# Four small re-orderings in a four-layer gated cross-attention kernel: a copy moved in ScalarE's queue, two PSUM tiles taken from another pool, the last additions reordered with one on GpSimd, and one split moved behind a transpose

## The chip, the cores and the metric

The kernel runs on one core of one Trainium2 chip, in one launch. The metric is device microseconds (us) from the start of the execution to its end; of three timed executions the median counts. The core has a matmul engine (TensorE, PE in the profile; its weight loads are listed apart as PEld), VectorE (DVE), ScalarE (ACT), GpSimd (POOL), and SyncE (SP), which here only issues DMAs. Every engine works through its own list of instructions in order, and waits at an instruction until the semaphores that it names have been counted up by others.

## The reference

Two batches of 256 tokens with 256 features (512 tokens in all, four tiles of 128) pass through four layers, each of them a gated cross-attention to a context of 512 rows per batch and then a gated feed-forward:

```python
x = x + tanh(g_xattn[l]) * xattn_l(layernorm(x), ctx)
x = x + tanh(g_ffn[l])   * ffn_l(layernorm(x))
```

Layer 0 has 16-head attention without projections and a feed-forward with ternary weights; layer 1 has 16 heads of width 128 with query, key, value and output projections, and a dense gated feed-forward; layer 2 has linear attention and a mixture of 8 experts of which each token uses one; layer 3 has one-head attention with a mask, and a mixture of 8 experts of which each token uses two (160 slots per expert), beside a shared feed-forward that all tokens use. Everything is float32.

## The kernel before

The 512 tokens live in one SBUF tile `x` of 128 partitions by four tiles by 256 features. The whole kernel is one straight program. Its engines' orders are set partly by the text (the helpers `inline`, with the lists `line`, `pool_line` and `pe_line`, keep DVE's, POOL's and PE's instructions of a stretch in the order in which the text writes them), partly by a scheduler that fills in the rest, and in places by `behind(i, j, reason)`, which tells the scheduler to place instruction `i` after instruction `j` on the same engine, without a semaphore. Tiles come from pools; a pool gives out a buffer again once its last readers are done, so a new tile makes its first writer wait for them. The PSUM pools that matter here are `ps_acc` (2 buffers, tag `acc`), `ps_mm` (4 buffers, tag `mm`, taken by `mm()`) and `ps_tr` (2 buffers, tag `tr`).

Four places are touched.

**Context parts (lines 602 to 623).** For layer 1 the turned context `ctxT` is split into a rounded part `ctx_top` and the scaled rest `ctx_rest`, so that products of full precision can be built from faster matmuls. The generator `context_parts` does this in four pieces (two batches by two feature halves), one at a time, between other work. A piece is: DVE cuts the low bits off (`cut`), ACT copies the result to `ctx_top` (line 614), DVE takes the difference (line 618), ACT scales it into `ctx_rest[:, 0]` (line 619), and one step later DVE forms `ctx_rest[:, 1]` from it (line 621). The fourth piece falls into the change from layer 0 to layer 1, where PE turns the four normalized token tiles (line 255), ACT copies each to `xT` (line 792, `turned_x`), PE computes two heads' first keys (`whole_keys`, `keys_step`, with ACT's copies in lines 776 and 796), and then the first two query products, which read the whole of `xT`. The list `copied` holds the copy of the last turned tile; only `top` is put behind it.

**Layer 2's experts (lines 1586 to 1676).** Tokens are gathered into slots of 32 rows, four of which make a `quad`; there are six quads. The loop over `q` runs `l2_up(q)`, then for the quad before `l2_mask(q - 1)` and `l2_down(q - 1)`, then `l2_turn(q)`, then `homeward`, which sends finished quads' rows back to the tokens with matmuls into `y`. `l2_down` ends by splitting its result in two halves: DVE cuts `top2` (line 1621), ACT copies it (line 1623), DVE subtracts (line 1624). `l2_turn` has PE turn `h` into a `tr` tile and `evict` copy it to `hT` on DVE and ACT by turns (lines 203 to 206); for quad 5 it is ACT's turn.

**Layer 3's experts (lines 1930 to 2016).** Ten quads of 128 slots in five pairs. `l3_up`, `l3_turn` and `l3_down` follow each other; `l3_down(q)` accumulates in a tile `acc` of `ps_acc`, `evict` copies it to SBUF (DVE and ACT by turns), and GpSimd scatters the rows to a table `yg` in DRAM with an indirect DMA (line 1847). The last pair, quads 8 and 9, is followed on PE by `shared_down(0)` to `shared_down(3)`, the shared feed-forward's output for the four token tiles, also in `acc`.

**The end (lines 2016 to 2042).** Once all ten scatters have landed, four DMAs (two from SP's queue, two from ACT's) read the table back, for each token its two rows: `rows[n]`. DVE adds, for each token tile `n`, the shared part (`add_to_x(n, accs[n], gf(3))`) and, in `final(n)`, the two rows (k = 0 and 1) with their weights `kept`; tile 3's rows go through PE instead, with `spread`. `store(n)` issues the output's DMA from SP. After the last instruction each engine reads the flag `bad`, branches past a fallback that is not taken here, and meets the others at a barrier.

Of the kernel before, what the change touches and what calls it, by code (L numbers as in the profile page):

```python
# [17 lines left out]
F32 = mybir.dt.float32  # L18
# [3 lines left out]
AF = mybir.ActivationFunctionType  # L22
# [3 lines left out]
P = 128  # L26
NT = 4
D = 256
# [11 lines left out]
EPS = 2.0 ** -12  # L40
# [10 lines left out]
def flamingo(ctx: ExitStack, tc: tile.TileContext, a: dict, out: bass.AP):  # L51
    nc = tc.nc

    def pool(name, bufs, space=None):
        kw = {} if space is None else {"space": space}
        return ctx.enter_context(tc.tile_pool(name=name, bufs=bufs, **kw))
# [4 lines left out]
    q1 = pool("q1", 4)  # L61
    small = pool("small", 6)
    ps_acc = pool("ps_acc", 2, bass.MemoryType.PSUM)


    x = const.tile([P, NT, D], F32, name="x")
# [37 lines left out]
    def pair(i, name, dtype=F32):  # L104
        return slab.tile([P, 2, WCOLS], dtype, tag=f"p{i}", name=name)
# [84 lines left out]
    def gf(layer):  # L190
        return tg[:, 4 + layer : 5 + layer]


    def behind(i, j, reason):

        tc.add_manual_dep(i.ins, j.ins.name, mybir.DependencyInfo(
            mybir.DependencyClass.NoSync, mybir.DependencyReason.DATA), reason=reason)
# [24 lines left out]
    def inline(i, line=line):  # L222
        if line:
            if line[-1] is not None:
                behind(i, line[-1], "in the order of the text")
            line[:] = [i]
        return i

    def norm_stats(n):

        st = small.tile([P, 6], F32, tag="st", name="st", bufs=4)
        mv = small.tile([P, 2], F32, tag="mv", name="mv", bufs=4)
        rstd = small.tile([P, 1], F32, tag="rstd", name="rstd", bufs=4)
        inline(nc.vector.bn_stats(st, x[:, n, :]))
        inline(nc.vector.bn_aggr(mv, st))  # L235
        inline(nc.gpsimd.tensor_tensor(rstd, mv[:, 1:2], eps_ln, ALU.add), pool_line)  # L236
        inline(nc.gpsimd.tensor_tensor(rstd, rstd, less_half, ALU.pow), pool_line)
        return mv[:, 0:1], rstd
# [40 lines left out]
    def mm(shape=None):  # L279
        return ps_mm.tile(shape or [P, 512], F32, tag="mm", name="mm")  # L280
# [5 lines left out]
    def add_to_x(n, acc, scalar, cols=slice(0, D)):  # L286
        return inline(nc.vector.scalar_tensor_tensor(x[:, n, cols], acc, scalar, x[:, n, cols], ALU.mult, ALU.add))  # L287
# [230 lines left out]
    mixed, acc, es, stats = {}, {}, {}, {}  # L518
    for s in range(18):
        n = s // 4  # L520
# [21 lines left out]
        if s % 4 == 2 and s < 16:  # L542
# [4 lines left out]
            if n == 0:  # L547
                rest = [norm_stats(m) for m in (2, 3)]
# [45 lines left out]
    def cut(dst, src):  # L594

        return nc.vector.tensor_scalar(dst.bitcast(I32), src.bitcast(I32), -4096, None, ALU.bitwise_and)

    ctx_top = nat.tile([P, B, 2, M], F32R, tag="nat", name="ctx_top")
    ctx_rest = pair(3, "ctx_rest", F32R).rearrange("p i (b k m) -> p i b k m", b=B, k=2)
# [4 lines left out]
    def context_parts():  # L604

        w = pair(5, "ctx_w").rearrange("p i (b k m) -> p i b k m", b=B, k=2)
        for b in range(B):
            for k in range(2):
                last = yield
                src = ctxT[:, b, k, :]  # L610
                t, l = (w[:, i, b, k, :] for i in range(2))
                i = cut(t, src)
                behind(i, last, "in turn, where there is room")
                top = nc.scalar.copy(ctx_top[:, b, k, :], t)
                for c in copied:
                    behind(top, c, "not among the turned tiles")
                copied.clear()
                nc.vector.tensor_sub(l, src, t)
                nc.scalar.mul(ctx_rest[:, 0, b, k, :], l, 1.0 / EPS)
                last = yield  # L620
                i = nc.vector.tensor_sub(ctx_rest[:, 1, b, k, :], t, ctx_rest[:, 0, b, k, :].bitcast(F32))
                behind(i, last, "in turn, where there is room")
        yield
# [317 lines left out]
    for h in range(16):  # L941
# [9 lines left out]
        for b in range(B):  # L951
# [12 lines left out]
            if h and h % 2 == 0:  # L964
                if b == 0:
                    sums1 = l1_sums([totals.pop((h - 2 + i, c)) for i in range(2) for c in range(B)])
                else:
                    scale = l1_turned(sums1)
# [23 lines left out]
            if hl and g < 3:  # L992
                n = 2 * (hl - 1) + b
# [9 lines left out]
    scale = l1_turned(sums1, 3)  # L1003
# [4 lines left out]
    t = totals.pop((15, 1))  # L1008
# [15 lines left out]
    scale = l1_scales(sums, 2)  # L1024
# [282 lines left out]
    t = negatives(early)  # L1307
# [63 lines left out]
    def rtile(shape=(P, NT, E), dtype=F32):  # L1371
        return small.tile(list(shape), dtype, tag=f"r{len(shape)}", name="route", bufs=12)
# [47 lines left out]
    turned = [logits2(n) for n in range(2)]  # L1420
# [37 lines left out]
    turned = []  # L1458
# [42 lines left out]
    t, u = rtile(), place  # L1501
# [45 lines left out]
    t = rtile()  # L1547
# [52 lines left out]
    def l2_turn(q, h):  # L1600
        n = 4 if q < 5 else 2
        hT = q2.tile([P, n, P], F32, tag="q2", name="hT2")
        tr = ps_tr.tile([P, n, P], F32, tag="tr", name="tr")
        for c in range(n):
            inline(nc.tensor.transpose(tr[:, c, :], h[:, c * P : (c + 1) * P], ident), pe_line)
        evict(hT, tr)
        return hT

    def l2_down(q, hT):
        acc = ps_tr.tile([P, D], F32, tag="tr", name="acc2")  # L1610
        n = 4 if q < 5 else 2
        for c in range(n):
            for j in range(4):
                at = c if q < 5 else j % 2 * n + c
                inline(nc.tensor.matmul(acc[j * BLK : (j + 1) * BLK, :], lhsT=hT[:, c, j * BLK : (j + 1) * BLK],  # L1615
                                        rhs=dn2[home(q, j)][:, at * D : (at + 1) * D], start=(c == 0), stop=(c == n - 1)), pe_line)
        if q < 3:
            reload_dn2(q)

        top = q1.tile([P, D], F32, tag="q1", name="top2")  # L1620
        nc.vector.tensor_scalar(top.bitcast(I32), acc.bitcast(I32), -4096, None, ALU.bitwise_and)
        o = kept_back[q][:, 1, :].rearrange("p (i d) -> p i d", i=2) if q < 4 else q2.tile([P, 2, D], F32R, tag="q2", name="o2")
        nc.scalar.copy(o[:, 0, :], top)
        nc.vector.tensor_sub(o[:, 1, :], acc, top)
        return o
# [24 lines left out]
    hTs, os, backs = {}, {}, {}  # L1650
# [9 lines left out]
    for q in range(QUADS + 1):  # L1660
        if q < QUADS:
            h = l2_up(q)
        if q == 0:
            second_rows()
        if 1 <= q <= QUADS:
            backs[q - 1] = l2_mask(q - 1)
            os[q - 1] = l2_down(q - 1, hTs.pop(q - 1))

        if q == 5:
            dn3 = [load(half, f"l3_dn{k}") for k, half in enumerate(halves_of(5, "dn3"))]  # L1670
            sh = [load(half, f"l3_sh{k}") for k, half in enumerate(halves_of(0, "sh3"))]
            gu3 = [load(half, f"l3_gu{k}") for k, half in enumerate(halves_of(3, "gu3") + halves_of(4, "gu3"))]
        if q < QUADS:
            hTs[q] = l2_turn(q, h)
        if 2 <= q < QUADS:
            homeward([(q - 2, 0)])
        if q == 5:
            homeward([(0, 1), (1, 1)])
        if q == QUADS:
            homeward([(4, 0), (2, 1), (3, 1), (4, 1)])  # L1680
            load_table(AF.Exp, silus[0], "the table of exponentials")
# [114 lines left out]
    es, t = l3_exps(0, ps3[0])  # L1796
# [107 lines left out]
    kept = const.tile([P, 2, NT], F32, name="kept")  # L1904
# [8 lines left out]
    def shared_down(n, more=[]):  # L1913
        acc = ps_acc.tile([P, D], F32, tag="acc", name="acc")
        chain(acc, [(hS[c // 2][:, c % 2, n * P : (n + 1) * P], shd[:, c, :]) for c in range(6)] + more)
        return acc
# [5 lines left out]
    for g in range(5):  # L1922
        t = q4.tile([P, 2, D + 1], F32, tag="q4", name="xg_sb")
# [33 lines left out]
        return hT  # L1957

    def l3_down(q, hT):
        acc = ps_acc.tile([P, D], F32, tag="acc", name="acc")  # L1960
        for c in range(2):
            for j in range(4):
                e = (4 * q + j) * BLK // CAP
                dw = dn3[e // 4].rearrange("p (e c d) -> p e c d", e=4, d=D)[:, e % 4, c, :]
                inline(nc.tensor.matmul(acc[j * BLK : (j + 1) * BLK, :], lhsT=hT[:, c, j * BLK : (j + 1) * BLK], rhs=dw,
                                        start=(c == 0), stop=(c == 1)), pe_line)
        o = q2.tile([P, D], F32, tag="q2", name="o3")
        evict(o, acc)
        scatter(yg, slots[q // 2][:, q % 2, D : D + 1].bitcast(I32), o, 2 * T - 1, returned)
# [26 lines left out]
    hs, hTs = {}, {}  # L1996
# [20 lines left out]
    accs = [shared_down(n) for n in range(2)]  # L2017
    rows = []
# [4 lines left out]
        rows.append(o)  # L2023

    def final(n):
        for k in range(2):
            add_to_x(n, rows[n][:, k, :], kept[:, k, n : n + 1])

    def store(n):
# [2 lines left out]
    for n in range(2):  # L2032
        add_to_x(n, accs[n], gf(3))
    accs = [shared_down(2), shared_down(3, [(spread[:, k, :], rows[3][:, k, :]) for k in range(2)])]
    final(0)
    store(0)
    add_to_x(2, accs[0], gf(3))
    for n in (1, 2):
        final(n)
        store(n)  # L2040
# [659 lines left out]
```

## Time and profile before

| | |
|---|---|
| timed runs, median (lowest to highest) | 546.95 us (546.9 to 547.33) |
| profiled execution, its own time | 548.4 us |
| its span from the first to the last instruction | 546.7 us |
| mean clock granted to TensorE | 0.997 |
| PE busy | 535.6 us, 98% |
| DVE, ACT, POOL busy | 61%, 43%, 23% |

The profile has a page (busy times, the span in slices, the chain of work that ended last, the costliest groups of instructions) and answers on parts of the trace. In a row of the timeline the columns are start and duration in us, engine, line, operation, the tile written and the tiles read, shapes, and how many instructions of the same kind the row merges; in brackets is the engine's idle time before it, and what ended that. The end of a matmul is modelled. The names `l_`, `w`, `acc` and the like are the program's tiles without their numbers, so that `acc2`, for one, is shown as `acc`.

### The profile page before, as it was taken

The page shows a single profiled execution, that of the slowest core. Times are in us where ns is not written, and L with a number is a line of the kernel's source. Part 1 is how long each engine was busy: PE and PEld are TensorE (multiplying, and loading weights), DVE is VectorE, ACT ScalarE, POOL GpSimd, SP SyncE. Part 2 cuts the span into 40 slices and gives each one's busy share as a digit, 9 for nine tenths or more (in the row PEclk, how much of TensorE's full clock was granted, in tenths as well). Part 3 has the DMA queues.
Part 4 walks back from the last instruction along what each step waited for, and adds up shares of the span by engine and source line. Part 5 has one row for each costly group of instructions (what it writes and reads, how often), then busy time and mean ns, then how long its engine had stood idle before and what let it go on. Part 6 is the DMA issues. An engine that isn't in the chain of part 4 may idle for free.

```text
span 546.7 us, 8723 instructions
## 1 busy us (share of the span) xinstructions
PE 535.6 (98%) x3304; PEld 394.6 (72%) x3304; DVE 333.3 (61%) x778; ACT 237.4 (43%) x487; POOL 124.1 (23%) x228
## 2 busy tenths in 40 slices
PE   8999999999999999999999999999999999999995
PEld 6554774878888888887888888687776447884464
DVE  5999797745556454754547567765477526562323
ACT  7886465644354434444344533551333212421320
POOL 5676104111021110311012223212022002252150
PEclk9999999999999999999999999999999999999998
DMA  8920130000004000040000404699040899413013
GB/s 265 424 67 0 25 129 1 1 1 0 1 0 151 4 2 1 1 153 1 0 1 1 155 0 155 230 316 375 22 153 1 309 398 291 174 48 121 19 50 127
DMA packets 15528, 57.06 MB, mean 104 GB/s; under 512 B 2653, under 2 KB 5924, under 8 KB 12102
## 3 DMA queue, kind: packets, MB, share of 16 engines
q1 hardware_dynamic: 13718, 51.61, 26.0%
q0 software_dynamic: 1472, 4.28, 2.3%
q8 instruction: 28, 0.46, 0.4%
q10 hardware_dynamic: 288, 0.52, 0.3%
q14 instruction: 22, 0.18, 0.1%
HBM read 51.60 MB, written 5.25 MB: 104 GB/s over the span
## 4 chain that ended last, share of the span: by engine, by line
PE 85%; DVE 5%; DMA 3%; issue 2%; POOL 2%; ACT 1%; SPq 1%; POOLq 0%; DVEq 0%
PE mm L284 26%; PE acc L284 18%; PE mm L643 9%; PE mm L645 4%; PE mm L1589 4%; PE q L643 2%; PE s L464 2%; PE mm L1943 2%; PE acc L1615 2%; DMA w<-in_l_gate 2%; PE gu L643 2%; PE acc L476 1%; PE outT L720 1%; PE q L645 1%; PE mm L1413 1%
## 5 line engine op out<-in xcount | busy, mean ns | idle before, releaser
L284 PE MATMUL mm<-qT,kT 128*128 128x256 f32 x256 | 60.7, 381 | 0.0
L284 PE MATMUL acc<-e,v 128*128 128x256 f32 x256 | 60.6, 379 | 0.0
L284 PEld LDWEIGHTS mm<-qT,kT 128*128 128x128 f32 x256 | 48.1, 190 | 9.3 <-ACT oT L835 1.6
L284 PEld LDWEIGHTS acc<-e,v 128*128 128x128 f32 x256 | 48.3, 189 | 8.2 <-issue 0.4
L631 POOL TENSOR_TENSOR h_parts<-w,h_top 128x256 fp32r<-128x256 f32 x28 | 20.8, 744 | 139.9 <-PE acc L284 73.6
L824 ACT ACTIVATE e<-mm 128x512 f32<-128x512 f32 x64 | 38.1, 598 | 22.3 <-PE mm L284 22.1
L827 DVE TENSOR_TENSOR t<-e,e 128x512 f32<-128x512 f32 x32 | 22.1, 690 | 24.4 <-ACT e L824 24.2
L468 ACT ACTIVATE e<-s 128x512 f32<-128x512 f32 x64 | 32.9, 605 | 6.0 <-PE s L464 5.8
L236 POOL TENSOR_TENSOR rstd<-mv,eps_ln 128x1 f32<-128x1 f32 x31 | 6.8, 219 | 109.4 <-DVE mv L235 109.3
L648 ACT ACTIVATE v<-mm 128x512 f32<-128x512 f32 x24 | 14.3, 597 | 31.1 <-PE mm L645 31.1
L643 PE MATMUL mm<-ctx_top,h_parts 128*128 128x512 f32 x56 | 27.3, 488 | 0.0
L284 PE MATMUL acc<-w,oT 128*128 128x256 f32 x112 | 26.8, 381 | 0.1
L835 ACT COPY oT<-acc 128x256 f32<-128x256 f32 x32 | 11.9, 372 | 34.2 <-PE acc L284 34.2
L649 DVE SCALAR_TENSOR_TENSOR v<-mm,v 128x512 f32<-128x512 f32 x24 | 16.6, 692 | 16.6 <-ACT v L648 16.6
L648 ACT ACTIVATE kT<-mm 128x512 f32<-128x512 f32 x28 | 16.7, 598 | 20.5 <-PE mm L645 20.5
L287 DVE SCALAR_TENSOR_TENSOR x<-acc,gsum,x 128x256 f32<-128x256 f32 x56 | 23.6, 476 | 2.8 <-PE acc L284 2.2
L649 DVE SCALAR_TENSOR_TENSOR kT<-mm,kT 128x512 f32<-128x512 f32 x28 | 19.3, 688 | 6.7 <-ACT kT L648 6.7
L284 PEld LDWEIGHTS acc<-w,oT 128*128 128x128 f32 x112 | 20.1, 190 | 3.5 <-ACT oT L835 0.5
L643 PE MATMUL mm<-v_parts,ctx_top 128*128 128x512 f32 x48 | 22.2, 462 | 0.0
L464 PE MATMUL s<-w_q,ctx_nat 32*128 32x256 f32 x256 | 21.6, 401 | 0.5 <-ACT e L468 0.2
L643 PE MATMUL mm<-ctx_rest,h_parts 128*128 128x512 f32 x56 | 22.0, 393 | 0.0
L649 DVE SCALAR_TENSOR_TENSOR qT<-q,qT 128x512 f32<-128x512 f32 x14 | 9.7, 691 | 18.4 <-ACT qT L648 18.4
(438 smaller groups left out, 1180.6 us busy)
## 6 DMA issues: line engine op xcount, KB each, us to landing
gu<-in_l_gu_all SPq DMA_DIRECT2D x14, 1024.0 KB, 7.3
w<-in_l_all SPq DMA_DIRECT2D x4, 2048.0 KB, 8.4
dn<-in_l_dn_all SPq DMA_DIRECT2D x4, 1024.0 KB, 6.3
dn<-in_l_dn_all SPq DMA_DIRECT2D x6, 512.0 KB, 8.6
gu<-in_l_gu SPq DMA_DIRECT2D x4, 704.0 KB, 17.5
ctxT<-in_ctxT SPq DMA_DIRECT2D x4, 512.0 KB, 11.6
ctx_nat<-in_ctx SPq DMA_DIRECT2D x3, 512.0 KB, 7.9
dn<-in_l_dn SPq DMA_DIRECT2D x2, 704.0 KB
```

The costliest lines, as they stand in the source:

```text
L284: inline(nc.tensor.matmul(dst, lhsT=lhsT, rhs=rhs, start=(i == 0), stop=(i == len(pairs) - 1)), pe_line)
L287: return inline(nc.vector.scalar_tensor_tensor(x[:, n, cols], acc, scalar, x[:, n, cols], ALU.mult, ALU.add))
L464: in_turn(nc.tensor.matmul(ps[j][:, k, :], lhsT=ctx_nat[rows, b, hf, c * P : (c + 1) * P], rhs=qm[rows, n, i, :], start=True, stop=True))
L468: exps.append(nc.scalar.activation(es[j], ps[j], AF.Exp))
L631: nc.gpsimd.tensor_sub(dst[1], src, t)
L643: inline(nc.tensor.matmul(same, lhsT=left(i, k), rhs=right(i, k), start=(k == 0 and i == 0), stop=(k == 1 and i == 1)), pe_line)
L645: inline(nc.tensor.matmul(cross, lhsT=left(2, k), rhs=right(2, k), start=(k == 0), stop=(k == 1)), pe_line)
L648: nc.scalar.mul(dst, cross, -EPS * scale)
L649: return inline(nc.vector.scalar_tensor_tensor(dst, same, (1.0 + EPS) * scale, dst, ALU.mult, ALU.add))
L824: nc.scalar.activation(e, s, AF.Exp)
L827: nc.vector.tensor_add(t, es[0], es[1])
L1589: inline(nc.tensor.matmul(ps[j * BLK : (j + 1) * BLK, :], lhsT=xsT[k][:, block * BLK : (block + 1) * BLK], rhs=gu2[home(q, j)][:, at : at ...
```

## The change

1. In `context_parts` the difference and the scaling into `ctx_rest[:, 0]` are written ahead of the loop over `copied`, and the scaling too is put `behind` the copies of turned tiles. In the built program ACT's order changes for the fourth piece alone: the scaling moves from between the second and third `xT` copies to behind the fourth copy and the `ctx_top` copy, past three copies. DVE's order is the same.
2. `l3_down` takes its tile from `mm()` for quads 8 and 9, and from `ps_acc` for the others, as before. PE's order is the same; the waits of the first matmuls of quad 8, quad 9, `shared_down(0)` and `shared_down(1)` change with the buffers.
3. At the end, `add_to_x(2, ...)` (the shared part of tile 2) is written ahead of `final(0)`; `final` takes k = 1 before k = 0; and for tile 2, k = 1, ACT scales the row into a new tile `row2` and GpSimd adds that to `x`. DVE has one instruction fewer, ACT and POOL one more each.
4. `l2_down` now returns its PSUM tile, and the split in halves is a function of its own, `l2_halves`. For all quads it follows at once, but for quad 4 it follows `l2_turn(5)`. On ACT, the copy of the turned tile of quad 5 now stands before the copy of quad 4's half; DVE's order is the same.

```diff
@@ context_parts
                 top = nc.scalar.copy(ctx_top[:, b, k, :], t)
+                nc.vector.tensor_sub(l, src, t)
+                rest = nc.scalar.mul(ctx_rest[:, 0, b, k, :], l, 1.0 / EPS)
                 for c in copied:
                     behind(top, c, "not among the turned tiles")
+                    behind(rest, c, "not among the turned tiles")
                 copied.clear()
-                nc.vector.tensor_sub(l, src, t)
-                nc.scalar.mul(ctx_rest[:, 0, b, k, :], l, 1.0 / EPS)
@@ l2_down
         if q < 3:
             reload_dn2(q)
 
+        return acc
+
+    def l2_halves(q, acc):
         top = q1.tile([P, D], F32, tag="q1", name="top2")
...
@@ the loop over quads
-            os[q - 1] = l2_down(q - 1, hTs.pop(q - 1))
+            acc = l2_down(q - 1, hTs.pop(q - 1))
+            if q != 5:
+                os[q - 1] = l2_halves(q - 1, acc)
...
         if q < QUADS:
             hTs[q] = l2_turn(q, h)
+        if q == 5:
+            os[q - 1] = l2_halves(q - 1, acc)
@@ l3_down
-        acc = ps_acc.tile([P, D], F32, tag="acc", name="acc")
+        acc = ps_acc.tile([P, D], F32, tag="acc", name="acc") if q < 8 else mm([P, D])
@@ final
-        for k in range(2):
+        for k in (1, 0):
+            if (n, k) == (2, 1):
+                t = q1.tile([P, D], F32, tag="q1", name="row2")
+                nc.scalar.activation(t, rows[n][:, k, :], AF.Copy, scale=kept[:, k, n : n + 1])
+                nc.gpsimd.tensor_add(x[:, n, :], x[:, n, :], t)
+                continue
             add_to_x(n, rows[n][:, k, :], kept[:, k, n : n + 1])
@@ the last additions
     accs = [shared_down(2), shared_down(3, [(spread[:, k, :], rows[3][:, k, :]) for k in range(2)])]
+    add_to_x(2, accs[0], gf(3))
     final(0)
     store(0)
-    add_to_x(2, accs[0], gf(3))
     for n in (1, 2):
```

## The prediction

> **What bounds the kernel.** I read the page first (busy times, then the chain that ended last), then the timeline around each of the four edits.
>
> ```profile
> span 546.7 us, 8723 instructions
> PE 535.6 (98%) x3304; PEld 394.6 (72%) x3304; DVE 333.3 (61%) x778; ACT 237.4 (43%) x487; POOL 124.1 (23%) x228
> ...
> PE 85%; DVE 5%; DMA 3%; issue 2%; POOL 2%; ACT 1%; SPq 1%; POOLq 0%; DVEq 0%
> ```
>
> PE is busy for 535.6 of 546.7 us, and the chain is PE's for 85%. So a gap closed in PE's row ahead of the last stage moves everything behind it, as long as nothing with a time of its own stands there. In the busy times by stage, PE has 229.92 of the 230 us from 100 to 330 us, and 41.83 of the 42 from 420 to 462. From 519.6 us on the chain leaves PE: scatters on POOL, their landing, the rows' DMAs, DVE's additions, the stores. There PE's gaps are worth nothing by themselves.
>
> The timeline of the first place:
>
> ```profile
> 89.35 0.37 ACT L792 COPY xT<-tr 128x256 f32<-128x256 f32 x1 [0.44 <-PE tr L255]
> 90.01 0.75 PE L255 MATMUL tr<-ident,xn 128*128 128x128 f32 x4
> 90.59 1.88 PE L284 MATMUL mm<-ctxT,w 128*128 128x512 f32 x4
> 91.30 0.63 ACT L619 ACTIVATE ctx_rest<-ctx_w 128x512 fp32r<-128x512 f32 x1 [1.58 <-DVE ctx_w L618]
> 91.83 0.57 ACT L796 COPY kT<-mm 128x512 f32<-128x512 f32 x1
> 92.30 0.65 ACT L792 COPY xT<-tr 128x256 f32<-128x256 f32 x2
> 93.00 1.12 PE L284 MATMUL q<-xT,w 128*128 128x512 f32 x2 [0.53 <-ACT xT L792]
> ```
>
> ACT stands idle for 1.58 us at the scaling of the fourth piece, which waits for DVE, while the third and fourth tiles, turned by 90.76, stay uncopied behind it, and PE at last waits for the copies.
>
> The second place, quad 4 and quad 5 of layer 2:
>
> ```profile
> 454.99 0.96 PE L1643 MATMUL y<-back 128*128 128x256 f32 x6
> 455.39 0.41 ACT L1623 CAST o<-top 128x256 fp32r<-128x256 f32 x1 [1.15 <-DVE top L1621]
> 455.71 0.36 ACT L206 COPY hT<-tr 128x256 f32<-128x256 f32 x1
> 456.12 1.07 PE L1615 MATMUL acc<-dn,hT 128*32 128x256 f32 x16 [0.17 <-ACT hT L206]
> ```
>
> ACT copies the half first, though the tile that PE waits for was turned earlier (454.80 + 0.44 = 455.24 in the same timeline).
>
> The end:
>
> ```profile
> 526.53 0.42 DVE L204 COPY o<-acc 128x256 f32<-128x256 f32 x1 [1.51 <-PE acc L1965]
> 527.00 1.93 PE L1965 MATMUL acc<-dn,hT 88*32 88x256 f32 x32 [0.36 <-DVE o L204]
> 528.50 0.97 POOL L1847 DMA_INDIRECT yg<-o,xg_sb  x1 [0.30 <-issue]
> 529.77 0.97 POOL L1847 DMA_INDIRECT yg<-o,xg_sb  x1 [0.30 <-issue]
> 530.72 0.37 ACT L206 COPY o<-acc 128x256 f32<-128x256 f32 x1 [3.63 <-remote]
> 531.36 0.97 POOL L1847 DMA_INDIRECT yg<-o,xg_sb  x1 [0.62 <-issue]
> 538.07 1.01 DVE L287 SCALAR_TENSOR_TENSOR x<-o3g,kept,x 128x256 f32<-128x256 f32 x2 [3.09 <-DMA o3g<-yg]
> 539.39 1.91 DVE L287 SCALAR_TENSOR_TENSOR x<-o3g,kept,x 128x256 f32<-128x256 f32 x4
> 541.22 0.48 DVE L287 SCALAR_TENSOR_TENSOR x<-acc,tg,x 128x256 f32<-128x256 f32 x1
> ```
>
> Scatters follow each other by 1.27 us (528.50, 529.77); only the last comes later, 1.59 us behind. Quad 9's eviction on ACT started at 530.72 though its matmuls end at 528.93 by the trace. I have no cause for these 1.8 us; other evictions start some 0.1 us after their matmuls.
>
> **Part 1, the scaling.** No work goes away; a 0.63 us scaling passes three copies on ACT. Before: four key matmuls from 90.59, pitch (1.88 - 0.59) / 3 = 0.43, so the first query matmul was due at 92.31; it came at 93.00, and its pair took 1.12 instead of 0.59 + 0.43 = 1.02. That is 0.69 + 0.10 = 0.79 us. After: ACT is free from 89.72; the `kT` copy waits for keys that end at 90.17, then two `xT` copies at the 0.28 between them: about 91.4, ahead of 92.31. So PE has no gap: **-0.79**. Bounds: the gap in the row alone, 0.53, and 0.79; I take 0.79, the distance of starts. What is late next: the scaling ends at about 92.45 instead of 91.93, and DVE's L621 waits for it. L621 already took 1.69 us there (0.684 in its median row), since POOL's subtraction ran from 91.83 for 1.27; it really could work only from 93.1 on, so 0.5 us later costs nothing. Behind it, DVE's first sum that PE needs (L827) starts at 100.42 after 1.23 us of idleness, which covers the 0.79. Nothing else with its own time stands in the way: the loads of that stretch were issued by 65.99 us and landed by 74.18.
>
> **Part 4, the halves.** The order on ACT is turned: the `hT` copy can start at 455.30 and ends at 455.66, and six `y` matmuls (last start 455.67, pitch 0.12) let PE go on at 455.79 instead of 456.12: **-0.33**. Bounds 0.17 (the gap in the row) and 0.33. The half of quad 4 is copied 0.3 us later, at about 456.03, and read by PE at 457.12 - 0.33 = 456.79: covered. DVE's order is unchanged. SP's loads of layer 3 follow PE here and landed by 471.75, far ahead of their use.
>
> **Part 2, the last experts.** Quad 8's matmuls no longer wait for quad 6's eviction (0.36 idle, 527.00 instead of about 526.46), `shared_down(0)` no longer for quad 8's; PE is 0.5 to 0.8 us earlier there, off the chain. On the chain, quad 8's scatter is bound by POOL's pitch from quad 6's (527.23), which does not move. Only the last scatter gains: 529.77 + 1.27 = 531.04 instead of 531.36, **-0.32**, if quad 9's eviction ends by 530.8; due at 528.46, it could again be 1.8 late (530.3 + 0.37) and still make it. Bounds: -0.32, and +0.6 if it is held until after the next scatter has been made (531.3 + 0.37 + 0.27 for POOL's start is 531.96).
>
> **Part 3, the last additions.** One 0.40 us step (the shared part of tile 2, at 539.00) moves ahead of the rows' landing, where DVE idles 3.09 us: covered. Another, 0.49 us, leaves DVE, and becomes ACT 0.4 (L1623's 0.41, a 128x256 cast) and POOL 0.73, the nearest row for an addition of this shape, L566:
>
> ```profile
> L566 POOL TENSOR_TENSOR all_r<-all_r,r x4: 727/730/1382, 27.9 to 55.5; 128x256 f32<-128x256 f32 x4
> ```
>
> Tile 2's row is the second DMA on SP's queue, issued at 534.69 and landing 3.7 to 4.5 us on, some 538.8; ACT ends at 539.25, POOL can start at about 539.4 to 539.5 (0.1 to 0.27 for a start behind a semaphore). DVE then runs tile 0 at 538.07 and 538.59, tile 1 at 539.00 and 539.50 to 539.99, all with two SBUF inputs. The maximum of the row above, 1382, lies beside such a DVE instruction, and L621 stretched to 1.69 beside POOL; so the two take turns. Either POOL goes second: 539.99 to 540.72, tile 2's last row at 540.79, tile 3's part at 541.19 (before: 541.22). Or first: tile 3's part at 540.99. **-0.1** between them. Bounds -0.55 (no turns taken) and +0.4 (POOL 1.38).
>
> The Trainium skill (SBUF — State Buffer, Who interferes with whom) says that a DVE instruction with two SBUF inputs and a GpSimd instruction that reads SBUF exclude each other for the whole instruction. By that rule part 3 is -0.03 to -0.2, without it -0.55; both rows agree with the rule.
>
> POOL's and ACT's exits are later by one instruction and have room: their last work stood at 531 and 535, the end at 546.7.
>
> **The sum.** 0.79 + 0.33 + 0.32 + 0.1 = 1.54 us. The profiled execution: 546.7 - 1.54 = 545.2 span, 548.4 - 1.54 = 546.9 of its own time. That execution stands 1.45 above the median of 546.95, so the median should be **545.4**. A change within 0.2% (1.09 us, 545.86 to 548.04) is about what can't be told from none here.
>
> **Rivals.** (a) *Gains swallowed.* One early gain is absorbed, or the last scatter does not come sooner: without part 1 the sum is 0.75 (546.2); without parts 2 and 3 it is 1.12 (545.8, on the edge); with the lower bounds throughout (0.53 + 0.17 - 0.6 - 0.4) about 547.2. For it: the unexplained late evictions at the end, and a chain that there hangs on POOL and DMAs. Against: PE at 229.92 of 230 us. (b) *Stores unblocked.* SP's issue of the third store took 1.30 us, against 0.34 for the first two, and the last store waited for it on SP: 542.72, though DVE was done at 541.70. If the earlier second store frees it, another 0.96 goes: 544.5. For it: only one of four was that long; against: I see no cause. (c) *Slower.* The same place the other way. If second, third and last issue take 1.30 each (2 x 0.96 more, counting 0.6 as short) and the last store lands 3.04 us after its issue, as the second did, not 1.95, the end is 1.9 + 1.1 = 3.0 later: 546.95 - 1.54 + 3.0 = 548.4. It decides from 2.6 us of such loss. For it: stores now leave closer together; against: they are issued by DVE's pace of 0.9 us or more. (d) *Part 3 without turns*: 0.45 more, 544.95.
>
> **How the numbers follow.** The forecast with its own spread (bounds of parts 1, 3 and 4; (d) in it) 0.57, range 544.9 to 545.9; (b) 0.12; (a) 0.26, of which a tenth beyond the edge of 545.86 on the fast side; (c) 0.05. Faster is 0.57 less a little at the edge, plus 0.12 and 0.03: 0.70; same 0.25; slower 0.05. From 544.4 to 546.6 less than 2 in 10 is left out: most of (c), the worst of (a), the best of (b).
>
> **What would show it.** Part 1: no gap ahead of the query matmuls, which start 0.43 behind the last key matmul, and L619's successor behind two `xT` copies. Part 4: `hT` before `o` on ACT, PE's quad 5 right behind the `y` matmuls. Part 2: ten scatters, the last four 1.27 apart. Part 3: POOL's addition of 0.73 or more, and a DVE row of line 287 stretched or shifted beside it; tile 3's part within 0.3 of its place relative to the rows' landing. The prediction is wrong if the end's start (the last scatter) does not come about 1.4 us earlier, or if SP's stores take another time than 4.2 us from the first to the last issue's end.

## The result, and the profile after

The changed kernel takes 546.13 us (median of 20 runs, 545.25 to 547.14) against 546.95 before (median of 20 runs, 546.45 to 547.6). The ratio is 0.9983, with a 95% interval of 0.9976 to 0.9990: 0.93 us faster, between 0.55 and 1.31. The forecast was 1.54. The time lies in the range that was given, the direction is right, and the gain is some 60% of the sum. By the forecast's own bound of 0.2% the median falls just inside "same", which had a chance of 0.25, and not in "faster", which had 0.70; the interval does exclude a ratio of 1.

The page of the changed kernel (span, busy times, chain of work that ended last):

```profile
span 543.5 us, 8726 instructions
PE 535.0 (98%) x3304; PEld 395.4 (73%) x3304; DVE 332.3 (61%) x777; ACT 238.1 (44%) x488; POOL 124.7 (23%) x229
...
PE 94%; DVE 3%; ACT 1%; issue 0%; POOL 0%
```

The two profiled spans differ by 3.2 us, far more than the times do. So the two profiles can't simply be subtracted; the places have to be read one by one. (Lines of the code that did not move are 1 to 13 higher in the changed kernel.)

The timeline of the first place, the scaling:

```profile
90.06 1.88 PE L284 MATMUL mm<-ctxT,w 128*128 128x512 f32 x4
90.16 0.65 ACT L793 COPY xT<-tr 128x256 f32<-128x256 f32 x2
90.69 0.64 ACT L614 CAST ctx_top<-ctx_w 128x512 fp32r<-128x512 f32 x1
91.21 0.65 ACT L616 ACTIVATE ctx_rest<-ctx_w 128x512 fp32r<-128x512 f32 x1
...
91.78 3.60 PE L284 MATMUL q<-xT,w 128*128 128x512 f32 x8
91.89 1.22 DVE L622 TENSOR_TENSOR ctx_rest<-ctx_w,ctx_rest 128x512 fp32r<-128x512 f32 x1 [0.49 <-ACT ctx_rest L616]
```

The two copies of turned tiles now come ahead of the scaling, and the query matmuls follow the key matmuls without a gap: 91.78 - 90.06 = 1.72 us from the first key matmul to the first query matmul, against 93.00 - 90.59 = 2.41 before.

The second place, quads 4 and 5 of layer 2:

```profile
453.45 0.44 PE L1606 MATMUL tr<-ident,h 128*128 128x128 f32 x2
...
453.64 0.95 PE L1647 MATMUL y<-back 128*128 128x256 f32 x6
...
453.93 0.37 ACT L206 COPY hT<-tr 128x256 f32<-128x256 f32 x1 [1.03 <-PE tr L1606]
...
454.19 0.41 ACT L1627 CAST o<-top 128x256 fp32r<-128x256 f32 x1
...
454.52 1.07 PE L1616 MATMUL acc<-dn,hT 128*32 128x256 f32 x16
```

`hT` is copied ahead of `o`, and PE's quad 5 follows the `y` matmuls with no idle time, 0.88 us behind the first of them instead of 456.12 - 454.99 = 1.13.

The end, in two windows of the timeline:

```profile
523.13 1.93 PE L1973 MATMUL acc<-dn,hT 88*32 88x256 f32 x32
...
524.88 1.91 PE L1973 MATMUL mm<-dn,hT 88*32 88x256 f32 x32
524.97 0.97 POOL L1855 DMA_INDIRECT yg<-o,xg_sb  x1 [0.62 <-DVE o L204]
...
528.80 0.97 POOL L1855 DMA_INDIRECT yg<-o,xg_sb  x1 [0.30 <-issue]
```

```profile
534.80 0.48 DVE L287 SCALAR_TENSOR_TENSOR x<-acc,tg,x 128x256 f32<-128x256 f32 x1 [2.10 <-PE acc L284]
535.20 1.91 DVE L287 SCALAR_TENSOR_TENSOR x<-o3g,kept,x 128x256 f32<-128x256 f32 x4
536.22 3.67 SPq L2043 DMA_DIRECT2D out_x<-x  x4
536.32 0.51 ACT L2037 ACTIVATE row<-o3g,kept 128x256 f32<-128x256 f32 x1 [9.09 <-DMA o3g<-yg]
536.91 0.78 POOL L2038 TENSOR_TENSOR x<-x,row 128x256 f32<-128x256 f32 x1 [7.14 <-ACT row L2037]
...
537.19 1.03 PE L284 MATMUL acc<-o3g,spread 128*128 128x256 f32 x4
537.73 0.48 DVE L287 SCALAR_TENSOR_TENSOR x<-o3g,kept,x 128x256 f32<-128x256 f32 x1 [0.62 <-POOL x L2038]
538.25 0.48 DVE L287 SCALAR_TENSOR_TENSOR x<-acc,tg,x 128x256 f32<-128x256 f32 x1
```

The chain of work that ended last runs over PE up to the last addition here, and no longer over scatters and DMAs (start and duration in us, merged; the first profile of before, then the changed kernel):

```profile
531.36 2.59 DMA yg<-o,xg_sb
...
534.25 3.73 DMA o3g<-yg
...
538.07 0.50 DVE x L287
```

```profile
526.79 11.44 PE acc L284 x52
538.23 0.03 issue
538.25 0.48 DVE x L287
```

No eviction is late in the changed kernel's profile, and the last scatter stands 528.80 - 523.13 = 5.67 us behind the first matmul of quad 6; in the profile of before it was 6.65 us. The question for the experiments is how much of that 1 us the change did.

### The profile page after: what moved, and what is told of

Its sections match the earlier page's. It is cut to its first block, busy times and chain, and to the rows that moved or that the text cites. A ratio compares the mean times of both kernels' runs of the same rounds, so it can differ in the third digit from the quotient of the medians.

```text
span 543.5 us, 8726 instructions
## 1 busy us (share of the span) xinstructions
PE 535.0 (98%) x3304; PEld 395.4 (73%) x3304; DVE 332.3 (61%) x777; ACT 238.1 (44%) x488; POOL 124.7 (23%) x229
## 4 chain that ended last, share of the span: by engine, by line
PE 94%; DVE 3%; ACT 1%; issue 0%; POOL 0%
PE mm L284 27%; PE acc L284 20%; PE mm L644 9%; PE mm L646 4%; PE mm L1590 4%; PE s L464 3%; PE acc L476 2%; PE q L644 2%; PE mm L1951 2%; PE acc L1616 2%; PE gu L644 2%; PE outT L721 1%; PE acc L1973 1%; PE q L646 1%; PE mm L1414 1%; PE y L1647 1%
```

## The experiments

Theory: the four terms add up (0.79, 0.33, 0.32, 0.10), and the missing 0.6 us lies in one of them. Rivals: an early gain is swallowed behind it; or the late evictions, from which part 2 was priced, are not in the executions that were timed. There are twelve runs in three groups, each group on a chip of its own (the expectations say "call" for a group). For the two first profiles the chip is not on record.

The table cuts the span of every profile at the same seven events (us; read from the traces, the rows add up to the span as the page rounds it): A start to the first of the four key matmuls; B to the first query matmul; C to the seventh of the ten scatters at the end (quad 6's); D to the tenth (quad 9's); E to the first addition of a gathered row; F to the addition of tile 3's shared part, the last on DVE; G to the end.

| kernel | chip | A | B | C | D | E | F | G |
|---|---|---|---|---|---|---|---|---|
| before, first profile | ? | 90.59 | 2.41 | 434.22 | 4.13 | 6.71 | 3.15 | 5.48 |
| changed, first profile | ? | 90.06 | 1.72 | 433.19 | 3.83 | 6.40 | 3.05 | 5.24 |
| e_again (before) | 1 | 90.52 | 2.41 | 433.55 | 3.83 | 6.50 | 3.15 | 5.54 |
| e_p14 | 1 | 91.39 | 1.72 | 433.19 | 3.83 | 6.22 | 3.23 | 5.12 |
| e_p23 | 1 | 90.19 | 2.41 | 433.57 | 3.83 | 6.39 | 3.05 | 5.26 |
| e_nogp | 1 | 90.34 | 1.72 | 433.20 | 3.83 | 6.48 | 2.97 | 5.16 |
| e_p1 | 2 | 90.17 | 1.72 | 434.10 | 4.16 | 6.34 | 3.15 | 5.56 |
| e_p2 | 2 | 90.46 | 2.41 | 434.27 | 3.84 | 6.42 | 3.15 | 5.66 |
| e_p3 | 2 | 90.28 | 2.41 | 434.24 | 4.16 | 6.27 | 3.00 | 5.74 |
| e_p4 | 2 | 92.56 | 2.41 | 433.98 | 4.17 | 6.53 | 3.15 | 5.29 |
| f_before (before) | 3 | 90.36 | 2.41 | 433.58 | 3.83 | 6.28 | 3.18 | 5.68 |
| f_all (changed) | 3 | 90.88 | 1.72 | 433.21 | 3.83 | 6.40 | 3.05 | 5.62 |
| f_nogp | 3 | 90.00 | 1.72 | 433.21 | 3.83 | 6.40 | 3.05 | 5.09 |
| f_nogp_acc | 3 | 90.06 | 1.72 | 433.17 | 3.83 | 6.39 | 3.05 | 5.27 |

B, C and D repeat to a few hundredths and change only with an edit, or with the late evictions; A, E and G scatter by some 0.5 us (A once by 2.2), in kernels that are equal there too. F must be read together with E: it starts at the first row's addition, which part 3 moves, and where E is short F is long (e_p14 and e_nogp). Parts 1, 2 and 4 are therefore read from B, C and D, and part 3 from E and F together.

**The kernel before, unchanged** (e_again):

> The kernel before, unchanged, as the measure of what two equal kernels differ by. Every theory: ratio 1 with an interval of some 0.1% to each side. For its profile: if the late evictions near the end (quad 6 by 0.7, quad 8 by 0.4, quad 9 by 1.8 us behind their matmuls) and the third store's issue of 1.30 us belong to the kernel, they are there again; if they belonged to that one execution, they are gone, the last scatter starts about 0.3 us earlier, and the span is nearer to 545.2 than to 546.7.

546.96 us against 546.85 for before in the same group, ratio 0.9993 (0.9980 to 1.0005). Its profile has no late eviction: C is 0.67 shorter and D 0.30 shorter than in the first profile, and its tail looks like that of the changed kernel. The same program has the late evictions in one execution and not in the other. So the first profile of before, 548.4 us, which is above every one of the 20 timed runs (547.6 at most), was not typical of them.

**Parts 1 and 4 alone** (e_p14), the hunks of `context_parts` and of `l2_halves` out of the change:

```diff
+                nc.vector.tensor_sub(l, src, t)
+                rest = nc.scalar.mul(ctx_rest[:, 0, b, k, :], l, 1.0 / EPS)
                 for c in copied:
                     behind(top, c, "not among the turned tiles")
+                    behind(rest, c, "not among the turned tiles")
...
+        if q == 5:
+            os[q - 1] = l2_halves(q - 1, acc)
```

> Parts 1 and 4 alone (the two that close gaps on TensorE). Sum of terms: 0.79 + 0.33 = 1.12 us faster (ratio 0.998). Rival, gains swallowed later: the query matmuls and quad 5 stand 0.8 and 1.1 us earlier in the profile, but the time moves by less than 0.6 us.

546.16 against 546.85, ratio 0.9983 (0.9971 to 0.9996): these two parts by themselves give as much as the whole change. B is 0.69 shorter and C 0.36; nothing behind them gives it back.

**Parts 2 and 3 alone** (e_p23):

```diff
-        acc = ps_acc.tile([P, D], F32, tag="acc", name="acc")
+        acc = ps_acc.tile([P, D], F32, tag="acc", name="acc") if q < 8 else mm([P, D])
...
-        for k in range(2):
+        for k in (1, 0):
+            if (n, k) == (2, 1):
...
+    add_to_x(2, accs[0], gf(3))
     final(0)
     store(0)
-    add_to_x(2, accs[0], gf(3))
```

> Parts 2 and 3 alone (the end). Sum of terms: 0.32 + 0.1 = 0.42 us faster (ratio 0.9992). Rival, the late evictions belonged to one execution and the last scatter was in step in most: nothing from part 2, and part 3 between 0.1 faster and 0.2 slower, ratio 0.9998 to 1.0004. If this rival and the terms of parts 1 and 4 hold, the whole change is worth about 1 us, as measured.

546.87 against 546.85, ratio 0.9997 (0.9985 to 1.0008). D is 3.83 with and without part 2. F is 0.10 shorter than in e_again and E 0.11; but E and F together are 9.44, and in e_p14, which has before's last additions, 9.45.

**The whole change with all rows of tile 2 on DVE** (e_nogp). Against the changed kernel:

```diff
-        for k in (1, 0):
-            if (n, k) == (2, 1):
-                t = q1.tile([P, D], F32, tag="q1", name="row2")
-                nc.scalar.activation(t, rows[n][:, k, :], AF.Copy, scale=kept[:, k, n : n + 1])
-                nc.gpsimd.tensor_add(x[:, n, :], x[:, n, :], t)
-                continue
+        for k in range(2):
             add_to_x(n, rows[n][:, k, :], kept[:, k, n : n + 1])
```

> The whole change, but the last row of tile 2 stays on VectorE (no scaling on ScalarE, no addition on GpSimd); the shared part of tile 2 stays ahead. By the terms of the prediction VectorE adds 0.49 us behind tile 2's other row: tile 3's part 0.1 to 0.3 us earlier or later than in the changed kernel, so the same within 0.05%. Rival, GpSimd and VectorE do not take turns: this kernel is 0.4 to 0.5 us slower than the whole change. Rival, the detour costs more than it saves: this one is 0.2 us or more faster than the whole change.

545.72 against 546.85, ratio 0.9975 (0.9964 to 0.9986). It is no slower than the changed kernel, so GpSimd's addition is not where the gain comes from; whether it is a loss is read on the third chip.

**Each part alone** (e_p1, e_p2, e_p3, e_p4; the edits are those shown, one at a time):

> Part 1 alone. Sum of terms: 0.79 us faster (ratio 0.9986), the query matmuls back to back 0.8 us earlier, and everything on TensorE up to the end as well. Rival, swallowed: the same 0.8 us at the queries, less than 0.4 in the time, and a gap later on TensorE that grew by the rest.

> Part 2 alone. Term of the prediction: 0.32 us faster, through the last scatter. Rival, the last scatter is already 1.27 us behind the one before it in most executions: same time within 0.1 us, with shared_down 0.5 to 0.8 us earlier on TensorE.

> Part 3 alone. Term of the prediction: 0.1 us faster (0.03 to 0.2 with turns between VectorE and GpSimd, 0.55 without). Rival (c), slower: stores closer together make SP's issues long, up to 1 us or more slower, with issues near 1.30 us in the profile.

> Part 4 alone. Term of the prediction: 0.33 us faster (0.17 to 0.33), quad 5's matmuls that much earlier. Rival, swallowed: 0.3 earlier at quad 5, nothing in the time.

| part | us, before 548.0 | ratio (95%) | in the profile |
|---|---|---|---|
| 1 | 547.29 | 0.9988 (0.9979 to 0.9997) | B -0.69, C -0.12 |
| 2 | 547.89 | 0.9996 (0.9987 to 1.0005) | D -0.30 |
| 3 | 547.87 | 0.9997 (0.9988 to 1.0006) | F -0.15 |
| 4 | 547.76 | 0.9998 (0.9989 to 1.0008) | C -0.24 |

The ratios of parts 2 to 4 are too small for the timing to tell from 1; the profiles carry them. No profile of before is from this chip, so C, D and F are set against the first profile of before, which has the late evictions too. Set against the other parts on this chip, C is 0.14 to 0.17 shorter with part 1 and 0.26 to 0.29 with part 4, and D is 0.32 shorter with part 2. Before takes 548.0 us on this chip, 1.15 more than on the first, and all four profiles have the late evictions. The timeline of part 1 alone on this chip, from quad 6 of layer 3 on:

```profile
523.49 1.93 PE L1966 MATMUL acc<-dn,hT 88*32 88x256 f32 x32
...
525.29 0.42 DVE L204 COPY o<-acc 128x256 f32<-128x256 f32 x1 [1.49 <-PE acc L1966]
...
525.77 1.93 PE L1966 MATMUL acc<-dn,hT 88*32 88x256 f32 x32 [0.35 <-DVE o L204]
525.99 0.97 POOL L1848 DMA_INDIRECT yg<-o,xg_sb  x1 [1.29 <-DVE o L204]
...
529.51 0.37 ACT L206 COPY o<-acc 128x256 f32<-128x256 f32 x1 [3.64 <-remote]
530.15 0.97 POOL L1848 DMA_INDIRECT yg<-o,xg_sb  x1 [0.64 <-issue]
```

and the same stretch of the kernel before on the third chip:

```profile
524.50 3.66 PE L1965 MATMUL acc<-dn,hT 88*32 88x256 f32 x64
...
525.64 0.42 DVE L204 COPY o<-acc 128x256 f32<-128x256 f32 x1 [0.83 <-PE acc L1965]
526.34 0.97 POOL L1847 DMA_INDIRECT yg<-o,xg_sb  x1 [0.62 <-DVE o L204]
...
528.23 0.37 ACT L206 COPY o<-acc 128x256 f32<-128x256 f32 x1 [1.35 <-PE acc L1965]
...
530.17 0.97 POOL L1847 DMA_INDIRECT yg<-o,xg_sb  x1 [0.30 <-issue]
```

The first eviction of quad 6 comes 1.80 us behind the start of its matmuls in the one, 1.14 in the other; the last scatter 6.66 and 5.67. In the second, quads 6 to 9 run as one block of 64 matmuls; in the first, PE stands for 0.35 in front of quad 8. Part 2 alone, on the chip with the late evictions:

```profile
524.61 1.93 PE L1965 MATMUL acc<-dn,hT 88*32 88x256 f32 x32
...
526.36 1.91 PE L1965 MATMUL mm<-dn,hT 88*32 88x256 f32 x32
...
529.91 0.37 ACT L206 COPY o<-mm 128x256 f32<-128x256 f32 x1 [2.93 <-remote]
530.97 0.98 POOL L1847 DMA_INDIRECT yg<-o,xg_sb  x1 [0.30 <-issue]
```

The eviction of quad 9 is still late, but early enough: the last scatter stands 6.36 us behind the start of quad 6, 0.30 less than 6.66. So part 2 does what the forecast said of it, where there is something for it to do.

**On the third chip: before, the change, and the change without GpSimd's addition, with and without part 2** (f_before, f_all, f_nogp; f_nogp_acc has in addition to e_nogp's edit):

```diff
-        acc = ps_acc.tile([P, D], F32, tag="acc", name="acc") if q < 8 else mm([P, D])
+        acc = ps_acc.tile([P, D], F32, tag="acc", name="acc")
```

> The kernel before once more, to see to what the late signals near the end belong. Five profiles so far have them (the seventh of the last ten scatters 2.26 to 2.29 us behind the sixth, the tenth 4.13 to 4.17 behind the seventh, unless quads 8 and 9 have other banks), five have not (1.60 and 3.83); the four of one call all had them, with a median of before of 548.0, the four of the other call none, with 546.85. Theory, they belong to the chip of a call: all four profiles of this call agree, and the median of before lies near 548.0 with them and near 546.9 without. Rival, they fall by chance on an execution: the four profiles differ.

> The changed kernel. By the terms as the profiles have them so far (part 1 0.80 and 0.12, part 4 0.24, part 3 0.10): 1.26 us faster than before without the late signals, and 0.3 more with them, ratio 0.9977 or 0.9971. Rival: as first measured, 0.9983, so that a third of a microsecond of these terms is lost somewhere.

> The change with VectorE adding all rows of tile 2, the shared part ahead. From its profile (tile 3's part 2.97 us behind the first row's addition, against 3.05 with GpSimd): 0.08 faster than the changed kernel, the same within what can be measured. Rival: really faster by 0.2 us or more, as the medians of the first call against the first measurement of the change suggest (545.72 and 546.13).

> As the one before it, without part 2 (quads 8 and 9 take the banks they had). If the late signals are not there, part 2 is worth nothing: the same time, with the last scatter 3.83 us behind the seventh. If they are, 0.3 us slower, with 4.15.

| kernel | us, before 546.81 | ratio (95%) |
|---|---|---|
| f_before | 546.91 | 1.0003 (0.9994 to 1.0012) |
| f_all | 545.81 | 0.9981 (0.9972 to 0.9990) |
| f_nogp | 545.75 | 0.9980 (0.9971 to 0.9989) |
| f_nogp_acc | 545.60 | 0.9981 (0.9972 to 0.9990) |

None of the four profiles has a late eviction, and before takes 546.81 us. Of 14 profiles, the five with late evictions are the four of one chip and the first of before; nine have none; none of the three chips has both kinds. That agrees with the theory that they belong to the chip, and with a median of before of 548.0 against 546.81 and 546.85. It is three chips, so it is not proved; and if the first profile of before came from the chip of its timed runs, which took 546.95, the theory would be wrong. Here neither part 2 nor GpSimd's addition is worth anything that the times can show. The end of the kernel without it:

```profile
535.16 2.83 DVE L287 SCALAR_TENSOR_TENSOR x<-o3g,kept,x 128x256 f32<-128x256 f32 x6
...
537.14 1.03 PE L284 MATMUL acc<-o3g,spread 128*128 128x256 f32 x4
538.21 0.48 DVE L287 SCALAR_TENSOR_TENSOR x<-acc,tg,x 128x256 f32<-128x256 f32 x1 [0.22 <-PE acc L284]
```

DVE does all six rows in one run and is done 0.22 us before it can go on: tile 3's part waits for PE's four matmuls over tile 3's rows. F is 3.05 with GpSimd and 3.05 without. Taking a row off DVE could gain nothing there.

## Why the prediction was right, and where its sum was too large

**Part 1, forecast -0.79: right.** B is 0.69 shorter in all seven profiles that have it, and the query matmuls keep a pitch of 0.43 (the third stands 0.86 behind the first instead of 0.96): 0.69 + 0.10, to the hundredth. What was late next was covered, as forecast: DVE's subtraction behind the scaling (line 621, now 622) ends 3.05 us behind the first key matmul, against 3.06 before (91.96 + 1.69 - 90.59). In both it ends some 0.55 us behind the first of the two subtractions that GpSimd makes beside it, and takes 1.22 and 1.69 us instead of the 0.68 of its other rows. The gain reaches the end: C does not grow by any of it.

**Part 4, forecast -0.33: the size was off, it measured about -0.25.** `hT` is copied in time (453.93 to 454.30), but the six `y` matmuls need 0.88 us up to the next matmul, not the 0.80 that the forecast took from their starts and a pitch of 0.12. PE has no idle time left there.

**Part 2, forecast -0.32: the term that failed, in the executions that were timed.** The mechanism was right (-0.30 to -0.32 where evictions are late); the condition was missing. The forecast read the 1.59 us between the last two scatters as a property of the kernel and said of the eviction 1.8 us late, "I have no cause". In nine of 14 profiles that lateness is not there and the last scatter follows at the 1.27 us pitch anyway. The step that failed is "That execution stands 1.45 above the median of 546.95, so the median should be 545.4": judged by e_again, most of these 1.45 us were C and D, 0.67 + 0.30 of lateness that the timed runs did not have, and a term priced in that stretch was carried over to them.

**Part 3, forecast -0.1: F is shorter by that much, but where no eviction is late the end is hardly earlier.** F is 3.00 to 3.05 instead of 3.15 to 3.23. With the row left on DVE it is 2.97 to 3.05 too, so it is the shared part of tile 2, moved ahead, that shortens F, and not GpSimd. But the cover of the moved step was not as wide as the 3.09 us of idle time said: DVE first waits 2.1 us for PE's sum, and the first row's addition stands right behind the part, 0.40 us later (534.80, 535.20). What F loses, E can gain. Six profiles without late evictions have the shared part ahead, and their E and F together are 9.44 to 9.45; three have before's last additions, with 9.45, 9.46 and 9.65. Some of them, in us behind PE's first matmul of `shared_down`:

| kernel | tile 0's rows landed | first row's addition | PE's matmuls over tile 3's rows | tile 3's part |
|---|---|---|---|---|
| e_again (before) | 8.49 | 8.58 | 10.46 | 11.73 |
| f_before (before) | 8.26 | 8.36 | 10.46 | 11.53 |
| e_p14 | 8.20 | 8.30 | 10.46 | 11.53 |
| changed, first profile | 8.28 | 8.48 | 10.46 | 11.53 |
| f_all (changed) | 8.37 | 8.48 | 10.46 | 11.53 |
| f_nogp | 8.30 | 8.48 | 10.46 | 11.53 |

In all nine PE has no gap from quad 6 on. Its four matmuls over tile 3's rows start at 10.46 although these rows landed at 9.36 to 9.64, and end at 11.49 by the trace; tile 3's part reads their sum. Two of the three profiles with before's last additions stand at that bound already, and part 3 could gain 0.20 in the third alone. The step of the forecast that does not hold here is "From 519.6 us on the chain leaves PE", with "There PE's gaps are worth nothing by themselves": that was read in the profile with late evictions, and without them PE's own run sets when the last addition starts, or comes within 0.2 us of it. Where evictions are late, E and F together were 9.27 with part 3 (e_p3) and 9.49 to 9.86 without it, in one profile against four.

The bound of -0.55 was out of reach whatever DVE and GpSimd do to each other; the forecast had not looked at what else tile 3's part waits for. The Trainium skill (SBUF — State Buffer, Who interferes with whom) gave turns as the rule for these two instructions. The addition took 0.72 to 0.78 us on GpSimd, DVE waited 0.62 to 0.68 for it, and the records overlap by only 0.1 to 0.2 us; the gain is the same either way, so no run decides it.

**The sum.** Where no eviction is late, B and C give 0.69 + 0.36 = 1.05 us, and E and F 0 to 0.2 more. The times gave 0.93 (0.55 to 1.31), in e_p14, which has parts 1 and 4 alone, 0.93 (0.22 to 1.59), and on the third chip 1.04 (0.55 to 1.53). All agree with 1.05. Of the 0.6 us by which the first measurement fell short, 0.32 is part 2, 0.08 part 4 and up to 0.10 part 3; the rest is inside the interval. The whole change was not timed on the chip with late evictions; there the parts add up to about 1.5 in the profiles (1.05, 0.30 and 0.15), which is a sum and not a measurement. That the time fell into the stated range is owed to the rivals in it: the forecast's own spread was 544.9 to 545.9, and 546.13 lies outside. Of its two signs of being wrong, both showed: the last scatter comes 1.05 us earlier (B, C and D against e_again), not 1.4, and the stores do not take 4.2 us.

**The rivals.** (a), gains swallowed, named the right outcome, "the last scatter does not come sooner", and nearly its price (545.8 without parts 2 and 3). For part 2 nothing was swallowed, the wait was simply not there; what part 3 gained on DVE was swallowed, behind PE. (b) and (c), SP's stores: the long issue of 1.0 to 1.4 us is on the third store in all three profiles of before (1.30, 1.42, 1.02) and on the fourth in both of the changed kernel (1.13, 1.19). It did not go. Nor is it shown that the change moved it: of the runs that have before's last additions, e_p1 and e_p4 have it on the third (1.10, 1.23) and e_p14 and e_p2 on the fourth (0.90, 1.74). The four issues take 3.67 and 3.73 us in the changed kernel and 4.21, 4.24 and 3.72 in before, so the 4.2 of the forecast is not kept; but G, 5.24 and 5.62, lies within the spread of the kernels that have before's last additions (5.12 to 5.68). Neither rival shows in the times.

## What to carry to other kernels

A wait in one profile for which no cause is found should be looked for in a second profile of the same kernel before anything is priced from it, all the more if that profiled execution is slower than every timed run. Cut the span at a few fixed events: stretches that repeat to hundredths show gains that are too small for the timing. But if an edit moves one of these events, read the stretches on both of its sides together: a gain in one can be lost in the other. And before work is taken off an engine, look at what else its next instruction waits for: here that was 0 to 0.2 us away.

## What the runs showed of the hardware

In all four profiles of one of three chips, and in the first profile of before, TensorE's signals came late at the same few places near the end. The matmul that ends the first half of the last gates (`mm<-gu,xgT`) has the same record in the first profile of before and in e_again (0.459 us long, starting at 520.40 and 520.33), but the semaphore event that it sends stands at 521.62 in the one and 520.83 in the other: 1.22 and 0.50 us behind its start, while the matmuls behind it keep their pitch. In the four other late profiles it stands 1.19 to 1.21 us behind. Later signals were up to 1.8 us late. Between these two profiles C and D differ by 0.97 us (0.67 and 0.30). The matmuls' own records do not show the delay; the semaphore events and the instructions that wait for them do. The Trainium skill (Perfetto Trace Analysis, Summary: the profiler window per engine type) says that the profile's end of a TensorE instruction is an estimate and that its signal is hidden; by that rule such a delay must be read from the instructions that wait, and the traces agree. The instruction stream was the same, the granted clock was 1.00 in these stretches in both kinds, and the loads of instructions that the trace shows nearby are in both. The cause stays open.
